# Block-sparse queries and keys projected without padding, each chunk written out twice with odd or even heads zeroed

## The chip, the cores and the metric

The kernel runs on one core of a Trainium2 chip. The metric is the device time of one execution in microseconds (us), the median of several runs. The engines are named as in the profile: PE multiplies matrices (PEld is its weight load), DVE is the vector engine, ACT the scalar engine, POOL the general engine, SP the queue from which most loads are issued.

## The reference, cut to what matters

The reference has two layers on an input of 8 x 512 x 256. Each layer adds two branches to its input, both fed from the same normalised input. The first layer is a state-space scan and a feed-forward part with four-bit quantised weights. The second layer is a block-sparse attention and a two-deep transformer with local attention. Only the block-sparse attention is touched here:

```python
# x: 8 x 512 x 256, 16 heads of 16, blocks of 128 tokens
q, k, v = heads(x @ w_qkv.T + b_qkv)
scores = q * 16 ** -0.5 @ k.T + mask      # own block, or block 0 on either side
out = softmax(scores) @ v
return out @ w_out.T + b_out
```

For four blocks the mask means that the queries of block 0 see all 512 keys, and those of block 1, 2 or 3 see block 0 and their own.

## The kernel before

The program has two stages, with all pools of the first released before the second. The first stage (the scan and the quantised feed-forward part) is not touched. In the second stage a Python loop runs over the 8 batches, and for each over the two depths of the local transformer. Its parts are generators that yield after each step, and `beside` (L111) weaves a second generator into the steps of a first: `beside(main, other, steps, others)` runs the other's steps spread over the main one's. Within this, the compiler of the tile language puts the instructions of each engine in one order ahead of time. PE follows the order of the code; DVE's and SP's orders can shift where the planner thinks an operand comes late. Each engine works its own list in order and waits on semaphores.

The order for batch b is (L929 to L936): local attention's projections `qkv(b, 0)` beside `st`, the block-sparse values for the first eight heads; `attn(b)` alone; `ffn(b, 0)` beside `smax(b, 1)`, the score maxima of the last eight heads; `qkv(b, 1)` beside `st(b, 1)`; `attn(b)` beside `proj(b + 1)`, the block-sparse projections of the next batch; `ffn(b, 1)` beside the maxima `smax(b + 1, 0)` and the output `outer(b)`. Only `proj(0)` and `smax(0, 0)` run alone, at the stage's start.

`proj` normalises the input (L520 to L524), transposes it (L529), and projects q and k transposed, channels on partitions (L534 to L542). The weights are padded on the host by `headed` (L950): each head of 16 channels takes 32 rows, the first 16 its channels, the 17th a spare row, the rest zeros. So q and k have 512 rows each, four chunks of 128 with four heads, one head to each group of 32 partitions. Each chunk is one PSUM bank: two matmuls (L538) over the 256 inputs, each executed as two passes in f32, so 4 passes, and one DVE write (L542) that adds the bias and scales q by 0.25. The spare row of k has the bias 1, that of q is 0. Values (L548 to L553) stay tokens on partitions.

`smax` (L559) takes two chunks at a time. For every block of queries it multiplies 16 rows of q with 16 rows of k in the four row groups of PE side by side (L581, L583), and DVE takes the negative maximum of each row (L587, L589) into a column of a tile `nm`. PE transposes `nm` (L570) and DVE adds it to q (L572), so that it lands in the spare rows. In `st` (L601) the scores are then computed again with keys on partitions, over all 32 rows, so that the spare rows subtract the maximum (L631, L633), ACT takes the exponential (L637), and PE multiplies with the values (L616, L618).

`attn` (L739) is the local attention in four pipelined steps of 8 units: scores L752 and L759, maxima on DVE L769, exponentials on ACT L775, scaling by the reciprocal sum L785 and L788, transposes L797, values L811. PSUM has six rotating banks (`pmm`), shared by all of these and by `proj`.

Of the kernel before, what the change touches and what calls it, by code (L numbers as in the profile page):

```python
# [9 lines left out]
FP = mybir.dt.float32  # L10
BF = mybir.dt.bfloat16
AF = mybir.ActivationFunctionType
ALU = mybir.AluOpType
AX = mybir.AxisListType
# [3 lines left out]
P = 128  # L18
NB, L, D = 8, 512, 256
NT = L // P  # L20
KC = D // P
# [6 lines left out]
NH, HD, HP = 16, 16, 32  # L28
# [10 lines left out]
def tile_kernel(ctx: ExitStack, tc: tile.TileContext, a: dict, out: bass.AP):  # L39
    nc = tc.nc  # L40
    pe, dve, act, pool, sp = nc.tensor, nc.vector, nc.scalar, nc.gpsimd, nc.sync
# [31 lines left out]
    def to_channels(x, dst, ptr, tag="tr"):  # L73

        for k in range(KC):
            ps = ptr.tile([P, L], FP, tag=tag, name="ps_tr")
            for t in range(NT):
                pe.transpose(ps[:, t * P : (t + 1) * P], x[:, t, k * P : (k + 1) * P], ident)
            evac(dst[:, k, :], ps)
# [31 lines left out]
    def beside(main, other, steps, others):  # L111

        at, other = 0, iter(other)
        for i, _ in enumerate(main):
            while at * steps < (i + 1) * others:
                at += 1
                next(other, None)
        for _ in other:
            pass

    def alone(strand):
        for _ in strand:
            pass
# [10 lines left out]
    def load(p, src, shape, name, eng=sp):  # L134
        t = p.tile(shape, FP, name=name)
        eng.dma_start(t, src)
        return t

    def chunks(w):
        return w.rearrange("(k p) n -> p k n", p=P)  # L140
# [4 lines left out]
    with ExitStack() as s0:  # L145
        w0 = s0.enter_context(tc.tile_pool(name="w0", bufs=1))
# [269 lines left out]
    with ExitStack() as s1:  # L416
        w0 = s1.enter_context(tc.tile_pool(name="w1", bufs=1, reuse_waits="tile"))
# [7 lines left out]
        def load_x1(b):  # L425
            t = w1.tile([P, NT, D], FP, tag="x1", name=f"x1s_{b}")
            sp.dma_start(t, x1_d[b])
            return t

        x1_first = load_x1(0)  # L430
        wq = load(w0, chunks(a["wq"]), [P, KC, NH * HP], "wq")
        wk = load(w0, chunks(a["wk"]), [P, KC, NH * HP], "wk")
        wv = load(w0, chunks(a["wv"]), [P, KC, D], "wv")
        bq = load(w0, a["bq"], [P, 4], "bq")
        bk = load(w0, a["bk"], [P, 4], "bk")
        bv = load(w0, a["bv"].unsqueeze(0).to_broadcast([P, D]), [P, D], "bv")
        wao = load(w0, chunks(a["wao"]), [P, KC, D], "wao")
        bsum = load(w0, a["bao"].unsqueeze(0).to_broadcast([P, D]), [P, D], "bsum")
# [4 lines left out]
        nms = [w0.tile([P, 2, P], FP, name=f"nm{i}") for i in range(NT)]  # L443
# [39 lines left out]
        S0 = 8  # L483

        def stream(name, tag="s"):
            s = w1.tile([P, KC, L + S0], FP, tag=tag, name=name)
            pool.memset(s[:, 1, S0 - 1 : S0], 0.0)  # L487
            return s
# [5 lines left out]
        def inv_sqrt(dst, src, bias=0.0):  # L494

            act.activation(dst, src, AF.Ln, bias=bias)
            act.activation(dst, dst, AF.Exp, scale=-0.5)

        def rows(g, n=HP):
            return slice(g * HP, g * HP + n)  # L500

        def both(x, j):

            return x.rearrange("p (j n) -> p j n", n=P)[:, 0 : j + 1 : j, :]

        def halves(x, i):
            return x[:, 2 * i * P : 2 * (i + 1) * P].rearrange("p (j n) -> p j n", n=P)
# [5 lines left out]
        def proj(b):  # L513
            x1 = x1s[b] = load_x1(b) if b else x1_first
            xn = one.tile([P, NT, D], FP, tag="hn", name="xn")
            st = sm.tile([P, NT, 6], FP, tag="ln_st", bufs=2, name="ln_st")
            mv = sm.tile([P, NT, 2], FP, tag="ln_mv", bufs=2, name="ln_mv")
            rs = sm.tile([P, NT], FP, tag="ln_rs", bufs=2, name="ln_rs")
            for t in range(NT):
                dve.bn_stats(st[:, t, :], x1[:, t, :])  # L520
                dve.bn_aggr(mv[:, t, :], st[:, t, :])
            inv_sqrt(rs, mv[:, :, 1], eps_t)
            for t in range(NT):
                dve.tensor_scalar(  # L524
                    xn[:, t, :], x1[:, t, :], mv[:, t, 0:1], rs[:, t : t + 1], ALU.subtract, ALU.mult
                )
            yield
            s = ss_[b] = stream("s0", "s0")
            to_channels(xn, s[:, :, S0:], pmm, "mm")  # L529
            yield  # L530
            qt = one.tile([P, 4, L], FP, tag="bqt", name="qt")
            kt = one.tile([P, 4, L], FP, tag="bkt", name="kt")
            bs[b] = qt, kt
            for dst, wt, bias, sc in ((qt, wq, bq, 0.25), (kt, wk, bk, 1.0)):  # L534
                for c in range(4):
                    ps = pmm.tile([P, L], FP, tag="mm", name="ps_qk")
                    for k in range(KC):
                        pe.matmul(  # L538
                            ps, wt[:, k, c * P : (c + 1) * P], s[:, k, S0:],
                            start=(k == 0), stop=(k == KC - 1),  # L540
                        )
                    dve.tensor_scalar(dst[:, c, :], ps, bias[:, c : c + 1], sc, ALU.add, ALU.mult)  # L542
                    yield
            for t in range(0, NT, 2):
                ps = pmm.tile([P, L], FP, tag="mm", name="ps_v")
                for i in range(2):
                    for k in range(KC):
                        pe.matmul(  # L548
                            ps[:, i * D : (i + 1) * D], s[:, k, S0 + (t + i) * P : S0 + (t + i + 1) * P], wv[:, k, :],
                            start=(k == 0), stop=(k == KC - 1),  # L550
                        )
                for i in range(2):
                    dve.tensor_tensor(  # L553
                        bv_t[:, t + i, :, :HD], ps[:, i * D : (i + 1) * D].rearrange("p (h d) -> p h d", d=HD),
                        bv.rearrange("p (h d) -> p h d", d=HD), ALU.add,
                    )
                yield

        def smax(b, p):  # L559

            qt, kt = bs[b][:2]
            cs = (2 * p, 2 * p + 1)
            back = []

            def to_rows(w):
                pt = pmm.tile([P, L], FP, tag="mm", name="pt_nm")
                for i in range(2):
                    pe.transpose(pt[:, i * P : (i + 1) * P], nms[w][:, i, :], ident)  # L570
                qw = qt[:, cs[0] : cs[0] + 2, w * P : (w + 1) * P]
                dve.tensor_tensor(qw, qw, pt[:, : 2 * P].rearrange("p (c n) -> p c n", n=P), ALU.add)  # L572

            for w, part in ((1, cs), (2, cs), (3, cs), (0, cs[:1]), (0, cs[1:])):
                banks = [pmm.tile([P, L], FP, tag="mm", name="ps_s") for g in range(4)]
                for i, c in enumerate(part):
                    for g in range(4):
                        q_ = qt[rows(g, HD), c, w * P : (w + 1) * P]
                        k_ = kt[rows(g, HD), c, :]
                        if w == 0:  # L580
                            pe.matmul(banks[g], q_, k_, start=True, stop=True)  # L581
                        else:
                            pe.matmul(halves(banks[g], i), q_, both(k_, w), start=True, stop=True)  # L583
                for g in range(4):
                    at = g * HP + HD
                    if w == 0:
                        dve.tensor_reduce(nms[w][:, part[0] % 2, at : at + 1], banks[g], AX.X, ALU.max, negate=True)  # L587
                    else:
                        dve.tensor_reduce(  # L589
                            nms[w][:, :, at], banks[g].rearrange("p (i n) -> p i n", i=2),  # L590
                            AX.X, ALU.max, negate=True,
                        )
                if back:
                    to_rows(back.pop())
                if part != cs[:1]:
                    back.append(w)
                yield
            to_rows(0)
            yield
# [329 lines left out]
        for b in range(NB):  # L929
            more = b + 1 < NB  # L930
            beside(qkv(b, 0), st(b, 0), 8, 7)
            alone(attn(b))
            beside(ffn(b, 0), smax(b, 1), 12, 6)
            beside(qkv(b, 1), st(b, 1), 8, 7)
            beside(attn(b), proj(b + 1) if more else (), 11, 12)
            beside(ffn(b, 1), chain(*([smax(b + 1, 0)] if more else []), outer(b)), 14, 18 if more else 12)  # L936


# [86 lines left out]
```

## Time and profile before

| | |
|---|---|
| median of 3 runs | 4067.31 us (4056.45 to 4068.78) |
| the profiled execution | 4060.3 us, span 4058.3 us |
| first pass of the block-sparse projections (L538) | at 1731.4 us of the span |
| PE busy | 3690.3 us, 91% of the span |
| DVE busy | 2647.0 us, 65% |
| ACT busy | 1724.7 us, 42% |
| POOL busy | 1326.4 us, 33% |
| mean granted PE clock | 0.91 |
| L538, q and k passes | 256, 126.0 us busy |
| L542, their DVE writes | 64, 47.7 us busy |

The span is cut into 40 slices of about 101 us on the page; the second stage begins within the 18th. A time in a list of stretches is counted from the span's start. A group's busy time counts overlapping instructions once; its mean is that of one instruction from start to end, so that pipelined passes of PE have a mean longer than their share of the busy time. What stands after the bar is the idle time of the engine just before the group, with the instruction that ended it.

### The profile page before, as it was taken

To read this page: it belongs to the slowest core of one execution; us is meant where nothing else is said; L and a number is where in the kernel's file an instruction comes from. 1 tells how busy PE (TensorE), PEld (TensorE's weight loads), DVE (VectorE), ACT (ScalarE), POOL (GpSimd) and SP (SyncE) were. 2 spreads that over 40 slices of the span, in tenths; PEclk is the share of its full clock that TensorE was granted. 3 is DMA by queue.
4 is the path that set the end of the run, shared out by engine and by line. 5 is a ranking of instruction groups with operands and counts; after the bars stand their busy time and mean duration, and the time that the engine had idled before them with its cause. 6 is when DMAs were issued, how large, how long until landed. Compare 5 with 4: busy or idle time off the path is not lost.

```text
span 4058.3 us, 41394 instructions
## 1 busy us (share of the span) xinstructions
PE 3690.3 (91%) x14428; PEld 1757.7 (43%) x14444; DVE 2647.0 (65%) x4809; ACT 1724.7 (42%) x3411; POOL 1326.4 (33%) x1059
## 2 busy tenths in 40 slices
PE   5889898898988988989999999999999999999998
PEld 1334343434343434344553554544544445445545
DVE  7877879787978787765654555555455456456444
ACT  3454646455645555433343243244234234333333
POOL 4555556555655555521012012021111101201210
PEclk7788789888988888989999999999989999999999
DMA  2111111111111111120011011011101111100100
GB/s 84 45 39 47 45 47 50 44 47 44 47 47 46 49 39 47 60 88 27 27 53 42 14 56 43 20 45 43 38 27 43 38 40 34 53 27 27 48 27 6
DMA packets 88712, 171.96 MB, mean 42 GB/s; under 512 B 10024, under 2 KB 41768, under 8 KB 88504
## 3 DMA queue, kind: packets, MB, share of 16 engines
q1 hardware_dynamic: 85568, 162.95, 12.5%
q10 hardware_dynamic: 2936, 6.36, 0.4%
q8 instruction: 115, 1.88, 0.2%
q14 instruction: 93, 0.76, 0.1%
HBM read 159.58 MB, written 9.70 MB: 42 GB/s over the span
## 4 chain that ended last, share of the span: by engine, by line
PE 46%; DVE 7%; issue 2%; ACT 2%; POOL 1%; DMA 0%; SPq 0%; POOLq 0%; DVEq 0%; ACTq 0%
PE ps_qkv L707 8%; PE ps_g L877 5%; PE ps_a L877 4%; PE ps_wo L839 3%; PE ps_qk L538 3%; PE ps_y L912 2%; PE ps_w L895 2%; PE ps_st L633 2%; PE lo L811 2%; PE pt_qk L698 2%; PE ps_ls L759 2%; DVE pr L788 2%; PE pt L797 1%; DVE nm L769 1%; PE ps_s L583 1%
## 5 line engine op out<-in xcount | busy, mean ns | idle before, releaser
L377 POOL TENSOR_TENSOR hh<-hh,cb 128x512 f32<-128x512 f32 x512 | 660.3, 1302 | 452.3 <-PE y L378 116.8
L378 PE MATMUL y<-hh,ident 128*128 128x512 f32 x1024 | 640.5, 740 | 126.3 <-POOL hh L377 123.5
L376 DVE TENSOR_TENSOR_SCAN hh<-da,hh 128x512 f32<-128x512 f32 x512 | 604.9, 1206 | 11.2 <-ACT da L374 11.1
L374 ACT ACTIVATE da<-delta,a_neg 128x512 f32<-128x512 f32 x512 | 348.7, 689 | 441.1 <-DVE hh L376 439.6
L378 PEld LDWEIGHTS y<-hh,ident 128*128 128x128 f32 x1024 | 202.5, 223 | 460.1 <-POOL hh L377 341.7
L369 DVE TENSOR_TENSOR hh<-du,bb 128x512 f32<-128x512 f32 x512 | 333.9, 672 | 71.7 <-PE bb L366 63.1
L366 PE MATMUL bb<-xd,sel 48*128 48x512 f32 x512 | 311.0, 710 | 26.6 <-DVE hh L369 26.6
L775 ACT ACTIVATE pr<-ps_ls,nm 128x256 f32<-128x256 f32 (+1 forms) x512 | 221.8, 446 | 174.9 <-DVE nm L769 174.7
L726 POOL TENSOR_TENSOR r<-r,r 128x512 f32<-128x512 f32 x128 | 162.8, 1272 | 355.4 <-DVE r L724 355.4
L884 DVE SCALAR_TENSOR_TENSOR ht<-ps_a,b,gl 128x512 f32<-128x512 f32 x96 | 71.9, 749 | 252.1 <-PE ps_a L877 252.1
L487 POOL MEMSET sa<- 128x1 f32 x16 | 1.6, 102 | 711.9 <-DVE sa L843 384.6
L722 DVE TENSOR_TENSOR r<-ps_qkv,tab 128x512 f32<-128x512 f32 x128 | 87.9, 687 | 222.1 <-ACT sq L721 222.1
L883 ACT ACTIVATE gl<-ps_g,b 128x512 f32<-128x512 f32 x96 | 65.9, 686 | 379.4 <-PE ps_g L877 379.4
L877 PE MATMUL ps_g<-hn,wf 128*128 128x512 f32 (+1 forms) x384 | 207.6, 659 | 20.5 <-issue 20.4
L721 ACT ACTIVATE sq<-ps_qkv 128x512 f32<-128x512 f32 x128 | 76.6, 598 | 272.9 <-PE ps_qkv L707 272.9
L877 PE MATMUL ps_a<-hn,wf 128*128 128x512 f32 (+1 forms) x384 | 191.2, 618 | 0.0
L366 PEld LDWEIGHTS bb<-xd,sel 48*128 48x128 f32 x512 | 89.5, 207 | 234.6 <-DVE hh L369 94.6
L637 ACT ACTIVATE pt_e<-ps_st 128x512 f32<-128x512 f32 (+1 forms) x384 | 172.8, 536 | 14.6 <-PE ps_st L631 13.8
L769 DVE TENSOR_REDUCE nm<-ps_ls 128x2 f32<-128x512 f32 (+1 forms) x256 | 147.4, 617 | 43.4 <-PE ps_ls L759 42.6
L707 PE MATMUL ps_qkv<-wqkv,s 128*128 128x512 f32 x384 | 174.9, 605 | 0.0
L707 PE MATMUL ps_qkv<-wqkv,sf 128*128 128x512 f32 x384 | 173.3, 601 | 0.0
L788 DVE TENSOR_SCALAR pr<-pr,lrs 128x256 f32<-128x256 f32 (+1 forms) x512 | 148.6, 332 | 4.8
(213 smaller groups left out, 6622.1 us busy)
## 6 DMA issues: line engine op xcount, KB each, us to landing
cb<-c_d SPq DMA_DIRECT2D x256, 256.0 KB, 3.1
wqkv<-in_wqkv SPq DMA_DIRECT2D x16, 1536.0 KB, 6.2
wf<-in_wf SPq DMA_DIRECT2D x16, 1364.0 KB, 11.0
wf<-in_wf SPq DMA_DIRECT2D x16, 768.0 KB, 4.7
tab<-tab SPq DMA_DIRECT2D x18, 512.0 KB, 6.9
wo<-in_wo SPq DMA_DIRECT2D x16, 512.0 KB, 3.9
x<-in_x SPq DMA_DIRECT2D x8, 512.0 KB, 4.0
x<-xs ACTq DMA_DIRECT2D x8, 512.0 KB, 2.8
```

Of the source, the lines that this page charges most:

```text
L366: pe.matmul(bb, sel[:, n, :], xd, start=True, stop=True)
L369: dve.tensor_tensor(hs[i], du[:, c0 + i, :], bb, ALU.mult)
L374: act.activation(da, delta[:, c, :], AF.Exp, scale=a_neg[:, c, n : n + 1])
L376: dve.tensor_tensor_scan(hh, da, hh, 0.0, ALU.mult, ALU.add)
L377: pool.tensor_tensor(hh, hh, cb, ALU.mult)
L378: pe.matmul(ys[i], ident, hh, start=(n == 0), stop=(n == NS - 1))
L637: act.activation(pt[:, :n], banks[g][:, :n], AF.Exp)
L707: pe.matmul(ps, shifted(s, k, t * P, P), wqkv[:, k, i * IN : (i + 1) * IN], start=(k == 0), stop=(k == KC - 1),)
L769: dve.tensor_reduce(nm, banks[r][:, : 2 * nk].rearrange("p (g n) -> p g n", g=2), AX.X, ALU.max, negate=True)
L775: act.activation(pr[:, at], banks[r][:, at], AF.Exp, bias=nm[:, i : i + 1], accum_out=rs[:, i : i + 1],)
L788: dve.tensor_scalar(pr[:, at], pr[:, at], rs[:, i : i + 1], None, ALU.mult)
L877: pe.matmul(dst[:m], wf1[:, k, off + c * P : off + c * P + m], hn[:, k, :], start=(k == 0), stop=(k == KC - 1),)
```

## The change

The host no longer pads q and k: the weights stay 256 wide, so that a bank holds eight heads of 16 rows. Each bank (4 passes) is written out by DVE twice, once with the odd heads zeroed and once with the even heads zeroed, by a multiplication with a column of ones and zeros (for q of 0.25 and zeros) and an added bias. So q and k still fill four chunks of 128 rows in SBUF, with one head to each group of 32 partitions, but the head lies in the upper or the lower half of its group. The first row of the zeroed half is the spare row; the bias of k is 1 there. The maxima multiply all 32 rows of a group, among them the spare row, where q is still 0. The maxima go to the columns of `nm` that answer to the new spare rows. The heads of v, of its bias and of the output weights are put into the order that the chunks now have. Two loads halve (wq, wk), one small load is new (`even`), and two small DVE operations at the stage's start make the scaled column and scale q's bias. The weave counts 8 steps of `proj` instead of 12.

```diff
-        wq = load(w0, chunks(a["wq"]), [P, KC, NH * HP], "wq")
-        wk = load(w0, chunks(a["wk"]), [P, KC, NH * HP], "wk")
+        wq = load(w0, chunks(a["wq"]), [P, KC, D], "wq")
+        wk = load(w0, chunks(a["wk"]), [P, KC, D], "wk")
...
+        even = load(w0, a["even"], [P, 2], "even")
+        evenq = w0.tile([P, 2], FP, name="evenq")
+        dve.tensor_scalar(evenq, even, 0.25, None, ALU.mult)
+        dve.tensor_scalar(bq, bq, 0.25, None, ALU.mult)
...
-        def rows(g, n=HP):
-            return slice(g * HP, g * HP + n)
+        def rows(g):
+            return slice(g * HP, (g + 1) * HP)
...
-            for dst, wt, bias, sc in ((qt, wq, bq, 0.25), (kt, wk, bk, 1.0)):
-                for c in range(4):
+            for dst, wt, bias, sc in ((qt, wq, bq, evenq), (kt, wk, bk, even)):
+                for j in range(KC):
                     ps = pmm.tile([P, L], FP, tag="mm", name="ps_qk")
                     for k in range(KC):
                         pe.matmul(
-                            ps, wt[:, k, c * P : (c + 1) * P], s[:, k, S0:],
+                            ps, wt[:, k, j * P : (j + 1) * P], s[:, k, S0:],
                             start=(k == 0), stop=(k == KC - 1),
                         )
-                    dve.tensor_scalar(dst[:, c, :], ps, bias[:, c : c + 1], sc, ALU.add, ALU.mult)
+                    for e in range(2):
+                        c = 2 * j + e
+                        dve.tensor_scalar(
+                            dst[:, c, :], ps, sc[:, e : e + 1], bias[:, c : c + 1], ALU.mult, ALU.add
+                        )
                     yield
...
-                        q_ = qt[rows(g, HD), c, w * P : (w + 1) * P]
-                        k_ = kt[rows(g, HD), c, :]
+                        q_ = qt[rows(g), c, w * P : (w + 1) * P]
+                        k_ = kt[rows(g), c, :]
...
-                    at = g * HP + HD
+                    at = [i * P + g * HP + (1 - i) * HD for i in range(2)]
+                    nm = nms[w].rearrange("p i n -> p (i n)")
                     if w == 0:
-                        dve.tensor_reduce(nms[w][:, part[0] % 2, at : at + 1], banks[g], AX.X, ALU.max, negate=True)
+                        i = part[0] % 2
+                        dve.tensor_reduce(nm[:, at[i] : at[i] + 1], banks[g], AX.X, ALU.max, negate=True)
                     else:
                         dve.tensor_reduce(
-                            nms[w][:, :, at], banks[g].rearrange("p (i n) -> p i n", i=2),
+                            nm[:, at[0] : at[1] + 1 : at[1] - at[0]], banks[g].rearrange("p (i n) -> p i n", i=2),
...
-            beside(attn(b), proj(b + 1) if more else (), 11, 12)
+            beside(attn(b), proj(b + 1) if more else (), 11, 8)
...
+    order = np.arange(NH).reshape(KC, 4, 2).transpose(0, 2, 1).ravel()
+    even = (np.arange(P)[:, None] // HD % 2 == np.arange(2)).astype(f)
+
+    def by_order(x):
+        return x.reshape(NH, HD, *x.shape[1:])[order].reshape(x.shape)
+
+    def parted(x, pad=0.0):
+        y = np.where(even[:, None, :] > 0, cols(x)[:, :, None], f(0.0))
+        y[0::HP, :, 1] = y[HD::HP, :, 0] = pad
+        return y.reshape(P, 2 * KC)
```

## The prediction

> **What bounds the kernel now.** I read the page first, then the stretches of the second stage, then the chain of waits inside one of them, then the groups by line and shape.
>
> ```profile
> PE 3690.3 (91%) x14428; PEld 1757.7 (43%) x14444; DVE 2647.0 (65%) x4809; ACT 1724.7 (42%) x3411; POOL 1326.4 (33%) x1059
> PE   5889898898988988989999999999999999999998
> DVE  7877879787978787765654555555455456456444
> PEclk7788789888988888989999999999989999999999
> ```
>
> From the 18th slice on, the second stage, PE is at nine tenths or more in nearly every slice, DVE near half. The change touches only this stage. Its q and k projections run once by themselves (batch 0) and seven times inside the second local attention of a batch. Four stretches: attention without projection, attention with it (both batch 1), the lone projection, the lone score maxima after it. Columns are length, then busy time of PE, PEld, DVE, ACT, POOL, then clock.
>
> ```profile
> 2101.70:2131.50 29.80, 28.65 (x248) 19.51 (x247) 24.35 (x77) 19.59 (x76) 0.00 (x0) 0.92 0.02 8
> 2232.40:2279.00 46.60, 46.45 (x305) 29.27 (x305) 33.46 (x88) 20.60 (x78) 0.00 (x0) 0.96 0.03 12
> 1731.40:1750.20 18.80, 18.80 (x48) 9.62 (x48) 7.66 (x18) 1.45 (x2) 0.72 (x1) 0.92 0.79 272
> 1750.20:1769.50 19.30, 16.81 (x76) 8.75 (x76) 15.81 (x34) 0.50 (x2) 0.00 (x0) 0.62 0.07 26
> ```
>
> With the projection PE idles 0.15 us of 46.60: every PE instruction there is on the path. Without it PE idles 1.15 of 29.80. The chain of waits inside the second stretch shows what a projection step costs (start, length):
>
> ```profile
> 2254.75 1.02 PE lo L811 x16
> 2255.78 1.91 PE ps_qk L538 x4
> 2257.69 0.43 PE ps_ls L752 x2
> ```
>
> Four passes L538 (an f32 matmul is two passes) take 1.91 us, not 4 x 0.43: the chain carries 0.2 us around the group. The groups, with busy time and mean of one:
>
> ```profile
> L538 PE MATMUL ps_qk<-s,wq 128*128 128x512 f32 x128 | 63.4, 622 | 0.5 <-DVE s L50 0.5
> L538 PE MATMUL ps_qk<-s,wk 128*128 128x512 f32 x128 | 62.6, 615 | 0.0
> L542 DVE TENSOR_SCALAR kt<-ps_qk,bk 128x512 f32<-128x512 f32 x32 | 24.0, 751 | 22.9 <-PE ps_qk L538 22.9
> L542 DVE TENSOR_SCALAR qt<-ps_qk,bq 128x512 f32<-128x512 f32 x32 | 23.7, 746 | 0.3 <-PE ps_qk L538 0.3
> ```
>
> And one line's durations (minimum, median, maximum) for 16 and for 32 rows contracted:
>
> ```profile
> L583 PE MATMUL ps_s<-kt,qt x768: 374/374/791, 1750.2 to 3894.4; 16*128 16x256 f32 x192
> L633 PE MATMUL ps_st<-qt,kt x768: 374/374/478, 1775.9 to 3956.7; 32*128 32x256 f32 x192
> ```
>
> **What the Trainium skill says.** *TensorE: Matmul & The Clock Gate*, section "LDWEIGHTS", says a weight load costs by its columns, not by the rows contracted. The trace agrees: 185 ns (L583, 16 rows), 184 ns (L633, 32 rows). *TensorEngine Tiling (Array Packing)*, "Key Properties", says that changing the tiling mode drains the array; the 0.2 us around each group, which lies between attention's 64-row or 64-column matmuls, fits that. *TensorE: Matmul & The Clock Gate*, "What's actually happening", says the clock halves after an idle window of about 3.4 us. The granted clock here is only ever 1.0 or 0.5, in multiples of 3.41 us, 225 us of half clock in the second stage. *VectorE: DVE Perf Modes*, "Why PSUM operands drop a tier", says f32 from PSUM runs at the base rate; L542 at 0.75 us for 512 columns agrees, so a second read of a bank costs as much as the first.
>
> **The change, part by part.**
>
> *PE passes removed.* Eight banks of q and k per batch become four, sixteen of 32 passes go. In attention that is four groups of 1.91 = 7.64 us a batch. The other passes (transposes, v) stay.
>
> *What the filler covered.* Eight projection steps are now spread over eleven attention steps; the built program has no filler after the last scores, before v. The stretch without filler shows such waits: 1.15 us, about 1.0 of it at that place, where values wait for the copied probabilities. I give back 1.1 a batch: 7.64 - 1.1 = 6.5, and seven batches make 45.8 us. Bounds: nothing given back (53.5); 4 us given back (25.5).
>
> *DVE writes.* There are still eight per batch, 128x512, but two from each bank, back to back, and with two per-partition operands. The nearest such form from PSUM is L268, 775 to 811 ns, against 746 to 751: 45 ns x 64 = 2.9 us at most, none at least. PE hides it: 33.5 of DVE in a stretch that shrinks to about 40. Without that cover it would cost 2.9 us in all. Each pair now holds DVE 1.5 us instead of 0.75; behind it stand the maxima L769, for which ACT's exponentials L775 wait, and behind those the transposes. A unit is then about 5.5 us of PE with a filler, against 3.05 + 1.5 of DVE, and results are wanted one unit later, so I charge nothing. If the pair did show, it costs 0.75 x 4 a batch. Half the banks, each held longer: six rotate, about five are taken per unit, so one is reused after more than 5 us against 1.5; nothing.
>
> *Score maxima.* The 256 + 768 passes of L581 and L583 contract 32 rows instead of 16: nothing, by the equal medians above. Results go to a stride of 112 instead of 128, same count: nothing.
>
> *The lone first projection.* 16 passes at 0.43 = 6.9 us go. Before: first pass 1731.4, first maximum L589 at 1753.64. After: four passes at half clock 3.4, twelve at 0.43 = 5.2, v 3.4, so PE reaches the scores at 1743.4. DVE starts writing at 1737.67 as before (it sits behind the mask casts, which wait for their load), eight writes 6.0 and v 1.5: 1745.2. The first maximum comes near 1745.5, 8.1 earlier. Batch 1's statistics, ahead of it before, are now among the maxima, DVE's own stretch (15.81 of 19.30), and give back about 2. That leaves 6.
>
> *Loads and two small DVE operations.* wq and wk are 512 KB less in all. The load of x1 now stands behind bq, bk and the new one, three issues of 0.6 us, and waits for b2l's landing: up to 2.4 us later than 1719.44; less data ahead of it gives back up to 1.9 at 272 GB/s. The two tiny operations stand before the batch statistics on DVE, wait for loads that are issued before x1 and cost about 0.2. The mask load moves about 0.4 us. I charge 1 for all (0 to 3). Left of the first projection: 5.
>
> Sum: 45.8 + 5 = 51 us. The profiled execution took 4060.3 (span 4058.3), the median is 4067.3, and the three runs spread over 12 us; I count from 4064, between the two. 4064 - 51 = 4013.
>
> **Rivals.**
>
> *A, softmax shows through (0.17).* The paired DVE writes delay the maxima by 0.75 in four units, and the drain by 1: 4 of 7.64 are given back, 25.5 + 4 = 29.5, so 4034. For it: DVE would be 33.5 of about 39, 86%, where attention alone idles PE at 82%. Against it: waits of attention alone total 1.15.
>
> *B, the clock helps (0.08).* Full 32-row strips in the score maxima, and fewer idle windows there, take away 40 us of the half clock, of which 156 lie in the feed-forward stretches with maxima: 40 us at half rate is 20 us more, 71 in all: 3993. Against it: those stretches idle on the layer norm's chain, which stays.
>
> *C, no gain in attention (0.07).* DVE and ACT pace it and the projection was free filler: 5 us, 4059. Against it: 46.45 of 46.60 busy.
>
> *D, slower (0.05).* The thinner attention lets the clock fall. A stretch of 3.41 us at half clock costs at most 1.7 us; 31 more undo the gain, over four per attention; six per attention make 7 x 6 x 1.7 = 71, so 4084. For it: the lone maxima at clock 0.62. Against it: attention without any filler kept 0.92.
>
> **How the numbers follow.** The forecast has 0.63, its own range 4000 to 4028 (40 to 60 us with the spread of runs). A, B and the forecast are faster: 0.88; C within: 0.07; D slower: 0.05. (0.3%, about 12 us, is what a measurement of this kernel can tell from no change.) The range runs from B's value to past A's: 3993 to 4040 leaves out part of B, C and D, with the tails of the rest under 0.2.
>
> **What would show it.** L538's successor: 128 passes, near 0.43 apart, PE busy down about 60. Attention with projection: 39 to 40 us, PE idle about 1. Score passes at 374 ns median with 32 rows. DVE writes 750 to 800 ns, still 64. First L707 after the lone projection 5 us nearer to the end of the first stage. The forecast is wrong if PE in that attention waits on L769, L775 or the pairs, or if half clock grows beyond 225 us.

## The result and the profile after

The changed kernel took 4013.39 us, the median of 4 runs (4003.5 to 4018.53), against 4068.05 for the kernel before on the same chip (4 runs, 4056.45 to 4071.02). The ratio is 0.9868, with a 95% interval of 0.9841 to 0.9895: about 54 us less, of 51 foretold. A second set of runs on another chip (e4 below) gave 4009.67 us and 0.9872 [0.9852, 0.9891]. The profiled execution after took 4003.5 us, its span is 4001.5. One execution of e8 below took 12267 us and is left out of its figures.

The page of the kernel after, the lines that answer to those of the prediction (busy time of each engine, then the 40 slices):

```profile
PE 3619.2 (90%) x14307; PEld 1729.1 (43%) x14316; DVE 2635.9 (66%) x4811; ACT 1725.4 (43%) x3411; POOL 1326.8 (33%) x1059
PE   5788989998988888989999999999999999999998
DVE  7887878787878787775645654555565456456444
PEclk7788898888888888899999999999999999999999
```

PE's busy time fell by 71 us, from 3690.3; the groups of the removed passes are 62 of it, by the rows shown below. DVE's hardly moved. The clock's row is all nines from the 18th slice on, where the row of before has an eight in the 18th and in the 30th. The clock is only ever 1.0 or 0.5; the trace has 232 us at half clock in the second stage of before (the prediction read 225) and 152 in that of after.

Stretches of the kernel after: attention without projection, three attentions with it, the lone projection, the lone score maxima behind it, and the first feed-forward part with maxima of batch 2 (columns: stretch, length, busy time of PE, PEld, DVE, ACT, POOL, then clock).

```profile
2094.90:2124.60 29.70, 28.37 (x250) 19.38 (x248) 24.62 (x77) 19.63 (x76) 0.00 (x0) 0.94 0.05 19
...
1943.70:1982.80 39.10, 38.62 (x290) 25.06 (x288) 32.71 (x90) 20.00 (x77) 0.00 (x0) 1.00 0.04 15
2785.50:2825.40 39.90, 39.47 (x290) 25.52 (x287) 32.34 (x90) 19.99 (x77) 0.00 (x0) 0.97 0.02 8
2504.30:2545.80 41.50, 41.36 (x290) 27.11 (x288) 32.85 (x90) 20.15 (x77) 0.00 (x0) 0.92 0.04 15
...
1742.80:1755.30 12.50, 12.50 (x36) 6.83 (x36) 7.86 (x18) 1.75 (x2) 0.72 (x1) 0.84 0.73 259
1755.30:1770.20 14.90, 14.50 (x73) 7.74 (x73) 12.81 (x26) 0.00 (x0) 0.00 (x0) 0.67 0.41 151
...
2404.70:2461.50 56.80, 52.02 (x170) 20.97 (x168) 24.47 (x41) 9.60 (x13) 2.58 (x3) 0.97 0.11 35
```

The same view of the kernel before, two stretches that the prediction did not show: the attention with projection that ran wholly at full clock, and a feed-forward part with maxima.

```profile
2811.90:2856.90 45.00, 44.85 (x305) 28.00 (x304) 33.31 (x88) 20.54 (x78) 0.00 (x0) 1.00 0.03 12
...
2420.60:2480.40 59.80, 56.21 (x170) 22.27 (x168) 24.49 (x41) 9.60 (x13) 2.58 (x3) 0.89 0.09 33
```

Two things are to be read here. An attention of before is 45.0 us at full clock and 46.6 with one clock window of 3.41 us at half rate (the prediction's stretch, 0.96): a window costs 1.6 us there. One of after is 39.1 at full clock, 39.9 with 2.3 us at half rate (0.97) and 41.5 with two windows (0.92). So at full clock an attention lost 5.9 us. And the feed-forward part, whose program did not change except for the rows of the maxima, is 3 us shorter where the clock is better; but either kernel has parts of about 57 and of about 60 us.

Summed over the batches, in us, with the half clock within:

| stretch | before | after | difference |
|---|---|---|---|
| end of the first stage to the first local projection | 41.1 | 35.2 | -5.9 |
| seven attentions with projection | 322.2 (15) | 282.1 (25) | -40.1 |
| eight feed-forward parts, first depth, with maxima | 470.3 (79) | 455.3 (31) | -15.0 |
| local projections, first depth | 350.4 (20) | 345.4 (7) | -5.0 |
| all the rest of the second stage | 1148.3 | 1148.5 | +0.2 |
| second stage | 2332.3 (232) | 2266.5 (152) | -65.8 |
| first stage, the same program in both | 1726.0 | 1735.0 | +9.0 |

The first stage, whose code is the same in all kernels here, took between 1725 and 1738 us in their profiles, so the 9 us are chance. 65.8 - 9.0 is the 56.8 between the two spans. How much of the 15 us of the feed-forward parts and of the 5 of the local projections is chance too, this pair of profiles can't tell; e1 and e3 below take that up.

The groups of the kernel after that the change touches, and the durations (minimum, median, maximum) of one line:

```profile
L545 PE MATMUL ps_qk<-s,wq 128*128 128x512 f32 x64 | 32.7, 639 | 0.1
L545 PE MATMUL ps_qk<-s,wk 128*128 128x512 f32 x64 | 31.4, 615 | 0.0
L551 DVE TENSOR_SCALAR kt<-ps_qk,even,bk 128x512 f32<-128x512 f32 x32 | 24.4, 804 | 0.4 <-PE ps_qk L545 0.4
L551 DVE TENSOR_SCALAR qt<-ps_qk,evenq,bq 128x512 f32<-128x512 f32 x32 | 24.3, 804 | 0.0
```

```profile
L594 PE MATMUL ps_s<-kt,qt x768: 374/374/792, 1755.3 to 3836.1; 32*128 32x256 f32 x192
```

128 passes are left, 64 us busy instead of 126. The writes take 804 ns instead of 749. A maxima pass takes 374 ns over 32 rows as over 16.

### The profile page after: what moved, and what is told of

It is laid out like the page before. It is cut to its first block, busy times and chain, and to the rows that moved or that the text cites. A ratio compares the mean times of both kernels' runs of the same rounds, so it can differ in the third digit from the quotient of the medians.

```text
span 4001.5 us, 41134 instructions
## 1 busy us (share of the span) xinstructions
PE 3619.2 (90%) x14307; PEld 1729.1 (43%) x14316; DVE 2635.9 (66%) x4811; ACT 1725.4 (43%) x3411; POOL 1326.8 (33%) x1059
## 4 chain that ended last, share of the span: by engine, by line
PE 38%; DVE 13%; ACT 3%; issue 2%; POOL 1%; DMA 0%; SPq 0%; POOLq 0%; ACTq 0%; DVEq 0%
PE ps_qkv L721 8%; PE ps_a L891 4%; PE ps_g L891 4%; PE ps_wo L853 3%; DVE pr L802 3%; DVE nm L783 3%; PE ps_y L926 2%; PE ps_w L909 2%; PE ps_st L647 2%; PE pt_qk L712 2%; ACT pr L789 2%; DVE nm L603 2%; PE o L632 1%; PE lo L825 1%; PE o L630 1%
## 5 line engine op out<-in xcount | busy, mean ns | idle before, releaser
L376 DVE TENSOR_TENSOR_SCAN hh<-da,hh 128x512 f32<-128x512 f32 x512 | 604.6, 1205 | 10.9 <-ACT da L374 10.8
L891 PE MATMUL ps_g<-hn,wf 128*128 128x512 f32 (+1 forms) x384 | 199.1, 636 | 25.1 <-issue 22.3
```

The costliest lines, as they stand in the source:

```text
L376: dve.tensor_tensor_scan(hh, da, hh, 0.0, ALU.mult, ALU.add)
L891: pe.matmul(dst[:m], wf1[:, k, off + c * P : off + c * P + m], hn[:, k, :], start=(k == 0), stop=(k == KC - 1),)
```

## The experiments

Ratios are to the kernel before on the same chip, with 95% intervals. The time at half clock is for a whole execution, twice the share that is missing to a mean clock of 1, averaged over the runs. Before has 727 +- 3, after 692 +- 9 and in e4 677 +- 11.

| | time, us | ratio | half clock, us |
|---|---|---|---|
| e1: before, maxima over 32 rows | 4055.79 | 0.9976 [0.9964, 0.9988] | 676 +- 4 |
| e2: after, passes run twice | 4066.43 | 1.0005 [0.9996, 1.0014] | 695 +- 3 |
| e3: before, writes issued twice | 4066.86 | 0.9999 [0.9989, 1.0009] | 720 +- 3 |
| e4: after, again | 4009.67 | 0.9872 [0.9852, 0.9891] | 677 +- 11 |
| e5: e1 in eight steps, count 8 | 4071.21 | 1.0016 [1.0003, 1.0030] | 711 +- 4 |
| e6: after, count 12 | 3988.39 | 0.9826 [0.9800, 0.9853] | 661 +- 5 |
| e7: after, output first | 4005.79 | 0.9862 [0.9837, 0.9888] | 681 +- 5 |
| e8: before, half the passes | 4019.60 | 0.9907 [0.9876, 0.9937] | 740 +- 13 |
| e9: after, filler late | 4001.34 | 0.9839 [0.9815, 0.9863] | 664 +- 6 |
| e10: after, joined start | 3995.83 | 0.9825 [0.9801, 0.9848] | 663 +- 4 |
| e11: e6 and e7 together | 3990.88 | 0.9818 [0.9793, 0.9842] | 651 +- 4 |
| e12: after, memset on DVE | 4011.06 (one run) | | |

### Are the passes the gain? (e2, e8)

My theory: the removed PE passes are the gain, the rest is small. Rival C: attention is paced by DVE and ACT. e2 puts the passes back into the changed kernel.

```diff
-                    for k in range(KC):
+                    for k in (*range(KC), *range(KC)):
                         pe.matmul(
                             ps, wt[:, k, j * P : (j + 1) * P], s[:, k, S0:],
```

> The changed kernel with the q and k passes of each bank run twice, the second overwriting the first, so that the number of passes is that of before; two DVE writes per bank, the 32-row maxima and the order of the heads stay. If the gain is the passes (forecast): about 50 us slower than the changed kernel, so within 0.4% of before. If a good part of the gain is the clock in the feed-forward stretches, from the 32-row maxima: 20 to 35 us slower than the changed kernel and still 0.5% faster than before. If attention had not been bound by PE (rival C): no change against the changed kernel.

It took 4066.43 us, ratio 1.0005: the gain is gone. Two attentions of e2, in the list of stretches:

```profile
2523.40:2571.40 48.00, 48.00 (x306) 30.12 (x303) 34.09 (x90) 20.15 (x77) 0.00 (x0) 0.93 0.03 11
1942.50:1987.50 45.00, 45.00 (x307) 28.12 (x305) 33.88 (x90) 20.00 (x77) 0.00 (x0) 1.00 0.03 12
```

The first is 48.0 us with PE busy throughout, against 41.5 for the stretch of after at nearly the same clock: 6.5 us for 16 passes, of 16 x 0.427 = 6.8. The second is at full clock and takes 45.0, as in the kernel before. The whole differs by 1.0005 - 0.987 = 0.0135, 55 us; seven attentions and the lone projection, 8 x 6.8, make 54.7. Rival C is out.

e8 leaves the kernel before as it is, but multiplies only half the inputs, so that its eight groups have two passes each.

```diff
-                    for k in range(KC):
+                    for k in range(1):
                         pe.matmul(
                             ps, wt[:, k, c * P : (c + 1) * P], s[:, k, S0:],
-                            start=(k == 0), stop=(k == KC - 1),
+                            start=(k == 0), stop=True,
```

> The kernel before with half of the q and k passes: it multiplies only the first 128 of 256 inputs, so q and k are not those of the reference. Eight banks of 2 passes, one write each, 16-row maxima, the weave of 12. This is the removal of passes alone: 16 of 0.43 us a batch, 6.9 x 8 = 55 us less what its filler covered. If that is all of the gain: 0.987 to 0.988 of before. If the 32-row maxima and their clock give some 9 us of it: 0.989 to 0.990.

0.9907 is 38 us less, with an interval of 25 to 50. In its profile the seven attentions fell by 43.4 us and the start by 5.6, together 49, although new idle time of 3.7 us stands before the masks' matmuls (L752). The rest of its second stage is within 2 us of that of before in sum; its first stage took 7 us longer, which is chance. So the removal of passes alone gains 25 to 50 us. The same number of passes was worth 55 us between e2 and the changed kernel, where the maxima have 32 rows and the weave counts 8. Whether the 17 us between the two are more than chance is not shown, and neither is a cause for them; the half clock of 740 +- 13 us can't be told from the 725 +- 5 of before on the same chip.

### Does the clock matter? (e1)

Rival B said that full 32-row strips in the maxima would raise the clock. e1 makes this edit alone, in the kernel before; the added rows hold the zero and the bias of the spare row, and zeros.

```diff
-                        q_ = qt[rows(g, HD), c, w * P : (w + 1) * P]
-                        k_ = kt[rows(g, HD), c, :]
+                        q_ = qt[rows(g), c, w * P : (w + 1) * P]
+                        k_ = kt[rows(g), c, :]
```

> The kernel before, with the score maxima alone contracting all 32 rows of a group instead of 16 (the other 16 are zero in q). If the rows cost nothing and do not move the clock (the forecast): the time of before within 0.3%, 374 ns median for L583, half clock in the second stage 216 us within 30. If full row groups keep the clock up (rival B): 10 to 20 us faster than before, and half clock in the second stage down by 40 to 80 us, most of it in the feed-forward stretches.

The ratio is 0.9976 [0.9964, 0.9988], 10 us less. A pass has the same median, 374 ns. The half clock falls from 727 to 676 us. In the two profiles PE, its weight loads, DVE and ACT work through the same instructions in the same order, so nothing but the rows differs. A feed-forward part of the second depth (batch 1), first in the kernel before, then in e1:

```profile
2279.00:2347.80 68.80, 65.16 (x242) 33.97 (x241) 29.49 (x55) 9.97 (x14) 4.85 (x7) 0.93 0.09 29
...
2280.40:2348.50 68.10, 64.35 (x242) 33.47 (x241) 29.30 (x55) 9.97 (x14) 4.86 (x7) 0.95 0.09 29
```

Seven of these eight parts hold maxima of the next batch. In the kernel before each of the seven has three windows at half clock, 10.2 us, and in e1, as in every other kernel here with 32 rows and this order, each has two, 6.8 us (e3 and e8, with 16 rows, have three in 13 of 14). The first depth's parts, which hold the other maxima, vary too much within one kernel to show the rows' share (56.8 and 59.6 us in e1). So the mechanism of rival B is real: the clock falls less often while these passes run. It is worth 10 us for 51 us of half clock, 0.2 us for one, and not the 0.5 that I reckoned. PE is not the bound in all of such a stretch: the seven parts take 477.1 us in e1 against 480.3, 3 us for seven windows, and PE idles 1.8 us more. The other 7 us are not found in one place: the first depth's parts take 468.2 us in e1, 470.3 in before, 463.4 in e3.

### Do the paired writes show? (e3)

```diff
+                    dve.tensor_scalar(dst[:, c, :], ps, bias[:, c : c + 1], sc, ALU.add, ALU.mult)
                     dve.tensor_scalar(dst[:, c, :], ps, bias[:, c : c + 1], sc, ALU.add, ALU.mult)
                     yield
```

> The kernel before, with each DVE write of a q or k bank done twice: 16 writes a batch instead of 8, back to back in pairs, 0.75 us more each. If DVE is covered by PE in that attention (forecast): within 0.3% of before, the attention with projection still 46 us. If pairs of writes show through in the softmax chain (rival A): 0.75 us for each of 4 to 8 pairs in seven batches, 21 to 42 us slower.

0.9999 [0.9989, 1.0009]. 64 more writes of 0.75 us, 48 us of DVE, cost nothing in the attention of before. This speaks against rival A's 29 us, though the attention of before is 6 us longer. Nor is there room for them in e2, which has the paired writes, an attention of 45.0 us and no idle time in it. What a pair does in the attention of after is seen next.

### What the count of the weave costs (e4, e5, e6, e9, e10)

The change also let the weave count 8 steps of `proj` instead of 12. With 8, the steps stand in attention steps 0, 1, 2, 4, 5, 6, 8 and 9; with 12 they would all stand in the first seven. e6 puts 12 back.

```diff
-            beside(attn(b), proj(b + 1) if more else (), 11, 8)
+            beside(attn(b), proj(b + 1) if more else (), 11, 12)
```

> The changed kernel with the weave counted as 12 of 11 instead of 8 of 11, so that its 8 projection steps come in the first attention steps and none in the last ones. If the waits that the filler covers lie at the end of attention (my step that gives back 1.1 us a batch): 3 to 8 us slower than the changed kernel. If PE has no such waits: the same within 0.2%.

It took 3988.39 us, ratio 0.9826, 17 to 19 us less than the changed kernel by the ratios. Neither of the two answers came. e4 is the changed kernel once more:

> The changed kernel once more beside the three others on one chip. Forecast: ratio to before 0.987 within 0.003. Its second profile tells which part of the first profile's picture repeats: attention with projection 39 to 41.5 us and 6 us from the last L399 to the first local projection should; a first stage 9 us longer and a half clock of 135 us in the second stage may not, if they are chance in where the clock's windows fall.

The ratio is 0.9872. In its profile the attentions with projection take 39.1 to 41.5 us again, and the first local projection starts 35.3 us after the end of the first stage. The longer first stage does not repeat (1725.2 us), and the second stage has 168 us at half clock.

e5 asks the same of a kernel with all its passes: e1 with two chunks to a step and the count 8.

```diff
-                    yield
+                    if c % 2:
+                        yield
...
-            beside(attn(b), proj(b + 1) if more else (), 11, 12)
+            beside(attn(b), proj(b + 1) if more else (), 11, 8)
```

> The kernel before with 32-row maxima, its projection woven in 8 steps instead of 12, two banks and 8 passes to a step, one DVE write per bank: the steps of the changed kernel with passes twice, without its paired writes. That kernel was at 1.0005 of before, the one with 32 rows alone at 0.9976. If the paired writes from one bank cost the 10 us between them: 0.9976 again. If the coarser weave costs them: 1.0005.

1.0016 against 0.9976 for e1: 16 us slower, though the work is the same. So the paired writes are not what separates e2 from e1, and eight coarse steps cost 16 us in a kernel with all its passes, too. Its half clock is 711 against 676 us, but its attention isn't longer at the same clock (46.4 us with one window, 46.6 in e1), so what costs there is not a wait in attention. e5 makes the steps coarser besides changing the count; e6 changes the count alone. The chain of waits inside an attention of the kernel after (start, length, instruction) shows one part of what it costs there:

```profile
2251.98 1.44 DVE kt L551 x2
2253.42 0.61 DVE nm L783
...
2254.12 1.93 ACT pr L789 x8
2256.05 0.48 ACT prt L52
2256.53 0.04 issue
2256.58 1.09 PE lo L825 x14
```

The pair of writes of the last k bank holds DVE for 1.44 us; a maximum of the last unit waits behind it, for that the exponentials, behind these on ACT the copy of the turned probabilities, and for the copy the values on PE. PE idles 0.33 us there (0.14 with two half-clock windows in the stretch), in each of the seven. The delay is larger than the idle time, since the ends of pipelined passes are modelled and run past the start of the next. PE's timeline of the attention at full clock has both (start, length):

```profile
1966.78 1.09 PE L825 MATMUL lo<-prt,lv 128*64 128x128 f32 x16
1967.81 1.98 PE L545 MATMUL ps_qk<-s,wk 128*128 128x512 f32 x4
1969.63 0.59 PE L766 MATMUL ps_ls<-mask,identb 128*128 128x512 bf16 x2
...
1974.29 0.43 PE L825 MATMUL lo<-prt,lv 128*64 128x128 f32 x2
1975.05 1.09 PE L825 MATMUL lo<-prt,lv 128*64 128x128 f32 x14 [0.32 <-ACT prt L52]
1976.07 1.99 PE L559 MATMUL ps_v<-wv,s 128*128 128x256 f32 x8
```

Sixteen values and the step to what follows take 1.03 us where nothing is waited for (1966.78 to 1967.81), and 1.78 behind the last scores (1974.29 to 1976.07). So PE loses 0.75 us there, about 0.55 where the stretch has two windows. That is rival A's mechanism, at less than 0.8 us a batch and not 4, and it stands before the values behind the last scores, where my prediction put a wait of 1.0. Two edits test it. e9 shifts the eight steps to attention steps 3 to 10, so that filler stands there:

```diff
-            beside(attn(b), proj(b + 1) if more else (), 11, 8)
+            beside(attn(b), chain((0, 0, 0), proj(b + 1)) if more else (), 11, 11)
```

> The changed kernel with the eight projection steps woven one to each of the last eight attention steps (3 to 10) instead of into steps 0, 1, 2, 4, 5, 6, 8 and 9, so that filler stands after the last scores. If my prediction put the uncovered waits at the right place (no filler at the end costs 1.1 us a batch), it gains about 7 us over the changed kernel: ratio to the kernel before 0.985. If instead it is the early filler that pays (the twelve-count weave, all filler in the first seven steps, gave 0.983), late filler is worse than the changed kernel: 4020 us or more, ratio 0.990 or above, with more PE idle or more half clock in the attention with projection.

e10 joins the norm and the transposes into one step. The transposes then stand in attention step 0, and q, k and v each come earlier (1, 2; 4, 5; 6, 8), so that no k pair stands in step 6. It moves two things at once, the transposes and the pairs.

```diff
-            yield
             s = ss_[b] = stream("s0", "s0")
             to_channels(xn, s[:, :, S0:], pmm, "mm")
```

> The changed kernel with the norm and the transposes of the projection in one step, so that the transposes come in attention step 0 as with the twelve-count weave, while the six matmul steps stay spread (1, 2, 4, 5, 6, 8) as with the count of eight. If the late transposes behind ACT's exponentials cost the time, it reaches the twelve-count weave: about 3990 us, ratio 0.983. If the even spread is what costs, it stays at the changed kernel: about 4010 us, ratio 0.987.

e9 gives 0.9839 and e10 0.9825. In neither does PE idle before the values; over the seven attentions PE idles 2.2 us in the kernel after, 0.7 in e9, 0.0 in e10 and e6. The attentions take 282.1 (283.3 in e4) us, 279.2 in e9, 276.9 in e10, 274.6 in e6. The list of stretches for e10, with one window:

```profile
2231.10:2270.60 39.50, 39.50 (x290) 26.37 (x287) 33.23 (x90) 20.15 (x77) 0.00 (x0) 0.96 0.04 15
```

and for e6 and e9, attentions at full clock:

```profile
3623.80:3661.70 37.90, 37.90 (x290) 25.16 (x288) 33.21 (x90) 20.16 (x77) 0.00 (x0) 1.00 0.04 15
...
1939.40:1978.50 39.10, 38.88 (x290) 25.34 (x288) 31.90 (x88) 20.47 (x78) 0.00 (x0) 1.00 0.04 14
```

So the place of the wait in my prediction was right: filler there takes it away (e9), and in e10, where no pair stands in front of the last maxima, PE doesn't idle there either. But late filler alone gains nothing in attention: at full clock one of e9 takes 39.1 us like one of the kernel after, since PE now idles in its first units, which have no filler. e9 and the changed kernel are not told apart by their intervals. In e6 an attention at full clock takes 37.9, so the count of 8 costs 1.2 us in it. The even spread itself costs next to nothing, since e10 keeps gaps in it and takes as long as e6 with one window (39.5). Whether e10's gain comes from the early transposes or from the pair's new place is not told apart. And the attention explains only 5 to 9 of the 17 to 19 us between the kernel after and e6 or e10. Another 3 to 8 stand in the second depth's feed-forward parts, 543.0 us (546.8 in e4) against 540.1 in e6 and 538.5 in e10, where PE idles 42.0 (44.9) us against 36.8 and 36.0; why it waits longer for the maxima there was not looked into. The half clock of the whole is 661 to 663 us in these two against 677 to 692, so the clock is a likely place for what remains, and this stays open.

### Can the second feed-forward part be had as well? (e7, e11)

e7 changes the order of what is woven into the second depth's feed-forward part.

```diff
-            beside(ffn(b, 1), chain(*([smax(b + 1, 0)] if more else []), outer(b)), 14, 18 if more else 12)
+            beside(ffn(b, 1), chain(outer(b), *([smax(b + 1, 0)] if more else [])), 14, 18 if more else 12)
```

> The changed kernel with the output of the block-sparse attention woven ahead of the next batch's score maxima in the second feed-forward part, instead of behind them. There PE now waits for the maxima on DVE during the layer norm, about 5 us a batch idle. If these waits are on the path and move off it: 10 to 20 us faster than the changed kernel, 0.983 of before. If the next step only waits for the maxima later, at the start of the next local projections: the same or up to 10 us slower.

The part itself lost 26 us (543.0 to 517.2), with a half clock of 5 us instead of 53. The whole gained nothing that can be measured: 0.9862. The seven attentions grew from 282.1 to 288.3 us with a half clock of 41 instead of 25, the local projections of the first depth by 10.9, the feed-forward parts of the first depth by 13.9. e11 puts this on e6.

> The twelve-count weave (3988 us, ratio 0.9826) with the output projection ahead of the score maxima beside the last feed-forward part. Alone, the second edit took 26 us out of that part and gave nearly all back in the attention and projections around it (4006 us, ratio 0.986 against 0.987). If what it gave back came from the attention's spread weave, the two together reach about 3975 us, ratio 0.979. If the give-back lies elsewhere (half clock that moves to other stretches), it stays at 3985 to 3992 us, ratio 0.982 to 0.983.

0.9818 against 0.9826: not told apart from e6. The attentions stay at 271.1 us this time, the feed-forward part at 524.5, the local projections are at 353.6 instead of 343.4. So e11 stays where the second answer put it, and the give-back isn't bound to the attention's weave. e6, e10 and e11 beat both kernels of the case, and no one of them beats the others.

### The two small DVE operations (e12)

In the prediction they cost 0.2 us together. The timeline of the kernel after at the second stage's start (start, length, engine):

```profile
1736.06 1.80 POOL L457 MEMSET bv_t<- 128x2048 f32 x1
1736.38 1.50 DVE L440 TENSOR_SCALAR bq<-bq 128x4 f32<-128x4 f32 x1 [0.66 <-DMA bq<-in_bq]
1736.72 1.17 DVE L439 TENSOR_SCALAR evenq<-even 128x2 f32<-128x2 f32 x1
```

Both end at 1737.88, just behind POOL's memset (1737.86), and batch 0's statistics stand behind them. In the profiles of e4, e6 and e9 too both end with the memset, whenever they began. e12 gives the memset to DVE, ahead of them.

```diff
-        pool.memset(bv_t, 0.0)
-        pool.memset(bv_t[:, :, :, HD : HD + 1], 1.0)
+        dve.memset(bv_t, 0.0)
+        dve.memset(bv_t[:, :, :, HD : HD + 1], 1.0)
```

> The changed kernel with the two memsets of the values' tile at the second stage's start issued on DVE instead of POOL, ahead of the two small operations on bq and even. In four profiles of changed kernels those took 1.2 to 1.6 and 0.8 to 1.2 us, and both ended within 0.03 us of the end of POOL's memset of 128x2048, whenever they had begun. If POOL's memset holds them up, they now take about 0.1 us each, though they come later by DVE's own memset (1 to 2 us). If they are slow in themselves, or wait for the loads of bq and even, they still take 0.8 us or more. The time of the whole cannot tell: 4000 to 4020 us by either.

The durations of the two lines in e12 (ns):

```profile
L440 DVE TENSOR_SCALAR bq<-bq x1: 126/126/126, 1734.7 to 1734.7; 128x4 f32<-128x4 f32 x1
...
L439 DVE TENSOR_SCALAR evenq<-even x1: 158/158/158, 1734.7 to 1734.7; 128x2 f32<-128x2 f32 x1
```

They take 126 and 158 ns: POOL's memset had held them. The Trainium skill states this in *SBUF — State Buffer*, "Who interferes with whom": a DVE `tensor_scalar` on SBUF can take the port pair that it shares with GpSimd, and the second to come waits for the whole instruction of the first. The start of the second stage is the same length in e12 (34.9 us against 35.2), since DVE now does the memset itself.

## Why the prediction was right, and where not

4013.0 was foretold and 4013.4 measured. The mechanism was right in its main term, the removed passes. That the number fits so closely is luck: the attentions gave 40 of 45.8 us, the maxima gave about 10 where nothing was charged, and the kernel before took 4068 us beside the changed one where the prediction counted from 4064.

*PE passes removed, 7.64 us a batch.* Right, and a little too large. e2 restores the time by restoring the passes. At full clock an attention goes from 45.0 us to 37.9 in e6, where PE doesn't idle: 7.1 of 7.64. The sixteen passes are 6.8 of it. From the first pass of a group to what follows PE's timeline has 1.82 us (1967.81 to 1969.63), and not the 1.91 that I took from the chain, so 0.11 us more than its four passes. That is behind values, which have 64 columns. The one group of the same attention that stands behind transposes, of 128 rows and 128 columns like its own, takes 1.72 (1948.66 to 1950.38). So the drain of which the Trainium skill speaks in *TensorEngine Tiling (Array Packing)*, "Key Properties", and on which I leaned for 0.2 us around a group, fits 0.1 us in it.

*What the filler covered, 1.1 given back.* Right in place and size, and not in its cause. At full clock an attention of after takes 39.1 us, 1.2 more than one of e6 and 5.9 less than one of before, of 6.5 foretold. 0.75 us are lost at the place named (values behind the last scores, waiting for the copied probabilities), and more in the first units. Ahead of the last maxima stood the paired write, which I had charged with nothing; in e6, where no pair stands there, values at that place still take 1.30 us (3657.49 to 3658.79), so the pair makes about half a microsecond of the 0.75. Over seven attentions the half clock rose from 15 to 25 us (28 in e4). 7 x 45.0 and 7 x 39.1 differ by 41.4, if the unrounded 45.03 and 39.12 are taken; 40.1 was measured (38.9 in e4), so the clock took one to three microseconds. That is the mechanism of rival D, a few per cent of its size. Of the 45.8, then, the smaller price of the groups took 3.5, the larger give-back 0.9 and the clock 1.3.

*DVE writes.* 804 ns, 64 of them, as bounded by the row of L268. 64 more of them cost nothing in e3; only the pair ahead of the last maxima shows.

*Score maxima: nothing.* This is the step that failed. Equal durations of one pass were not the whole cost of a pass: with 16 rows full clock is granted less often. e1 measures the term at 10 us (5 to 15 by its interval) in the kernel before; in the changed one it was not measured apart. About 3 of the 10 stand in the second depth's parts, of which seven have a window less each; the 15 us of the first depth's in the table can't be put down to the rows, since e3, with 16 rows, has 463.4 us there, and e1 468.2. I had it as rival B at 20 us, with a chance of 0.08, and argued against it that the layer norm's idle time would keep the clock low. The norm's idle time stayed, and the clock rose.

*Lone first projection, 6 less 1.* 5.9 us measured. The prediction's stretch of the lone maxima, to 1769.5 us, takes in 2.4 us of the local projection, which starts at 1767.1. The charge of 0.2 us for the small DVE operations should have been about 1.5, and the statistics of batch 0 start 2.6 us behind the last matmul of the first stage instead of 0.5; the lone passes and maxima gave more (18.8 to 12.5 us from the first pass of one to the first of the other, and 16.9 to 14.9 from there to the local projection).

The sum: 40 from attention, 10 from the maxima, 6 from the start make 56; 52 to 57 was measured. The prediction had 45.8, 0 and 5. The new count of the weave, which I took for a matter of 1.1 us a batch, is worth 17 to 19 us in the changed kernel: with 12 it takes 3988.

*The signs it named.* 128 passes, 64 writes near 800 ns, maxima at 374 ns, the first local projection 5.9 us nearer, half clock below 225 us: all as foretold. PE's busy time fell by 71 and not 60; in the second stage alone by 81 (2190.1 to 2109.1), where there is less half clock, while in the first it rose by 10 with that stage's length. Attention with projection: 39.1 to 41.5 us, mean 40.3, PE idle 0.3 instead of 1. One sign of being wrong came true in small: PE in that attention does wait on a pair.

## What to carry to other kernels

Where PE is busy in all of a stretch, removed passes come off the time one for one (7.1 us here for 6.8 of passes). Where a change holds an edit of the work and one of the schedule (here a count in the weave), cost the two apart: here the small one gave back a quarter of what the large one gained. And look at what stands on a queue ahead of the last unit's chain: one pair of writes there made PE wait, where 64 more writes in the kernel before did not. An idle time in a profile can be shorter than the delay that it stands for: 0.32 us for 0.75 here.

## What the runs showed of the hardware

*Rows and the clock.* The same passes with the same durations over 32 rows instead of 16 in each row group took the half clock of an execution from 727 +- 3 to 676 +- 4 us (e1), although the added rows hold zeros but for the spare row of k. The Trainium skill, in *TensorE: Matmul & The Clock Gate*, "What's actually happening", lets the clock depend on how busy PE was in a window; these runs show that rows count in it. In the second depth's feed-forward parts with maxima it is one window of three, in each of the seven. How rows count was not tried.

*Batches in step with the clock.* In e6 and e10 one batch follows the other mostly after 279.8 or 279.9 us, which is 82 times 3.413; in e1 they alternate between 290.1 and 286.7, 85 and 84 times. The kernel before and the changed one wander (287 to 293 and 278 to 282). In step, the batches have their windows at the same place: all seven attentions of e1 and the first six of e6 hold one. Out of step, the seven of the kernel after hold none, one or two. That an edit which moves work a little moves windows into a stretch or out of it, and that this is why e7's 26 us were lost again, is argued, not shown.

*A memset on another engine.* Two DVE operations of 0.13 and 0.16 us took 1.50 and 1.17 beside POOL's memset (e12).
